# A four-layer graph-attention kernel: the end of layer 2 without its division, other forms of small VectorE operations, and mean rows taken elsewhere

## The chip, the cores and the metric

The kernel runs on one core of one Trainium2 chip. The time is that of one execution on the device in microseconds, and the figure for a kernel is the median of its runs. A separate execution is recorded by the hardware profiler; all views of the profile come from that one.

The engines appear under these names: PE (TensorE, matrix products), PEld (its weight loads), DVE (VectorE), ACT (ScalarE), POOL (GpSimd) and SP (SyncE, which issues most DMAs). Each engine works through its own queue in order and waits at an instruction whose inputs are not there.

## The reference

Eight graphs' worth of node features `x` (8 × 2048 × 64) pass through four attention layers over one sparse 2048 × 2048 adjacency. Each layer adds its output to `x`, and reads `h = max(layernorm(x), 0)`:

```python
h = jnp.maximum(_layernorm(x, axis=-1), 0.0)
x = x + _L0_gnn_ref(h, adj)          # dot-product attention over h
h = jnp.maximum(_layernorm(x, axis=-1), 0.0)
x = x + _L1_gnn_ref(h, adj, W, a)    # additive attention, then elu
h = jnp.maximum(_layernorm(x, axis=-1), 0.0)
x = x + _L2_gnn_ref(h, adj, Wh, bh, Wo, bo, gamma, beta)
h = jnp.maximum(_layernorm(x, axis=-1), 0.0)
x = x + _L3_gnn_ref(h, adj, W, a)    # additive attention, then relu
```

Layer 2 has two attention steps. The second of them is what the text below calls "layer 2's end":

```python
h = jnp.einsum('bnc,hdc->bhnd', x, Wh)
out_h = _gat_layer(h, mask[None, None], bh[None, :, None, :])   # 4 heads
z = jax.nn.leaky_relu(cat, negative_slope=0.2)
h2 = jnp.einsum('bnk,dk->bnd', z, Wo)
out2 = _gat_layer(h2, mask[None], bo)                 # softmax(h2 h2^T) h2 + bo
z2 = jax.nn.leaky_relu(out2, negative_slope=0.2)
mu = jnp.mean(z2, axis=-1, keepdims=True)
var = jnp.mean(jnp.square(z2 - mu), axis=-1, keepdims=True)
out = (z2 - mu) * jax.lax.rsqrt(var + LN_EPS) * gamma + beta
```

## The kernel before

The nodes are cut into 16 tiles of 128. A row holds all eight batches of a node: 8 × 64 = 512 values (`F` = 512, `B` = 8, `D` = 64), so a tile is 128 x 512 in fp32. The graph is sparse, so the kernel first makes lists of neighbours from the adjacency (`lists`, in layer 0's stage), and each layer gathers the neighbours' rows from a table in DRAM by indirect DMA (`gather`, L244, issued by POOL) into a ring of 26 slots. A tile has `ROWS[i]` slots in which every node has its own neighbour and `PACKED[i]` slots in which the remaining edges of all its nodes are packed together. There are 49 and 32 of these, 81 in all. For packed slots two selection matrices, `sel` and its transpose `selt`, say to which node an edge belongs. `sel` is made in layer 0, stored to DRAM and, at layer 2's end, loaded back as one DMA of 2 MB (L880).

Each layer is a `pipeline` of stages over the tiles. Stages of different tiles are written out interleaved, and the framework's scheduler orders each engine's queue further by a timeline of its own. Buffers rotate (`bufs=`), so a stage can run ahead only as far as they allow.

The stages that matter for the change:

- `norm_a` and `norm_b` are the layer norm. `norm_a` sums the rows on DVE (L261), makes the mean (L265) and subtracts it (L268), both on an engine given as `eng`, and has ACT square the result. `norm_b` sums the squares (L281), and ACT makes the inverse root as exp(−0.5 · ln(q/D + eps)).
- `pre_c` makes the normalised row `xh` (ACT, eight instructions a tile, L292) and transposes it on PE (L300) with a copy by ACT (L301). `pre_d` multiplies it with `u` (L343) and stores the row to the next layer's table (`store_rows`, L352). For tables 0, 1 and 4, `store_rows` also adds the tile to a mean row: products with `ones` (L357), a DVE addition to `acc` (L361), and after the last tile a transpose, a copy and a DMA to row N of the table. The gathers of the next layer wait for all rows of the table, the mean row included.
- `scores` multiplies the query rows with gathered rows and sums over each head (L423, L425, L431, L432, all DVE). `exps` takes the exponentials on ACT (L437).
- `weigh_sum` multiplies the gathered rows with the weights, on POOL in layer 0 and at layer 2's end (L381), and sums the slots on PE into `y` in PSUM (L386).

At layer 2's end, `second3` adds up the weights S and takes 1/S (L902, L903). `third3` multiplies y by 1/S (L472), adds the bias `bo` (L910), takes the leaky relu (L445, L446) and starts the layer norm. `fourth3` scales (L292), multiplies by gamma (L918), adds beta (L919), adds x (L486), stores x, and starts the next layer's norm on DVE. At the end `bounds` keeps the largest S, which later decides whether the result is within the limits of this method.

In layer 0, POOL has the mean and the centring of the norm (L265, L268), the addition of the attention's result to x (L480), `weigh_sum` and the gathers. In the two additive layers (1 and 3) `weigh_sum` is on DVE, and POOL has the gathers and little more.

Of the kernel before, what the change touches and what calls it, by code (L numbers as in the profile page):

```python
# [65 lines left out]
def edge_stack(ctx: ExitStack, tc: tile.TileContext, x_in, adj, w1, w1t, a1, wh, wht, bh, wo, bo,  # L66
# [28 lines left out]
    nc.gpsimd.memset(eps, EPS)  # L95
    ones = const.tile([P, 1], F32, name="ones")
# [17 lines left out]
    acc = const.tile([P, F // P], F32, name="acc")  # L114

# [40 lines left out]
    bo_b, gamma_b, beta_b = (const.tile([P, D], F32, name=name) for name in ("bo_b", "gamma_b", "beta_b"))  # L156

    def weights_in(pool):
# [34 lines left out]
        for t, src in ((bo_b, bo), (gamma_b, gamma), (beta_b, beta)):  # L193
            nc.gpsimd.dma_start(out=t, in_=bass.AP(tensor=src.tensor, offset=src.offset, ap=[[0, P], [1, D]]))
# [60 lines left out]
    def rows_of(k, i):  # L255
        return table[k][i * P:(i + 1) * P, :F]

    def norm_a(src, st, centre, eng=nc.vector):
# [4 lines left out]
        if centre:  # L263
            mean = small.tile([P, B], F32, name="ln_m")
            eng.tensor_scalar(mean, s, INV_D, None, op0=OP.mult)  # L265
            st["less"] = None
            st["src"] = rows_pool[0].tile([P, F], F32, name="ln_xc", bufs=3)
            eng.tensor_tensor(heads(st["src"]), heads(src), wide(mean), op=OP.subtract)  # L268
# [4 lines left out]
        nc.vector.tensor_scalar(st["less"], s, -INV_D, None, op0=OP.mult)  # L273
# [4 lines left out]
    def norm_b(st):  # L278
# [3 lines left out]
        nc.scalar.activation(q, q, AF.Ln, scale=INV_D, bias=eps)  # L282
# [12 lines left out]
    def transposed(src):  # L295
# [5 lines left out]
        nc.scalar.copy(t.rearrange("p k n -> p (k n)"), p)  # L301
# [5 lines left out]
    def pre_c(u, eng=None):  # L307
        def f(i, st):
# [6 lines left out]
            if u is not None:  # L315
                st["xt"] = transposed(st["xh"])
# [19 lines left out]
    def pre_d(k, u):  # L336

        def f(i, st):
# [8 lines left out]
            store_rows(k, i, xh, k != 2)  # L347
        return f

    def store_rows(k, i, xh, mean):  # L350
        cols = table[k].shape[1]
        nc.sync.dma_start(out=table[k][i * P:(i + 1) * P, :], in_=xh[:, :cols])  # L352
        if mean:
            C = F // P
            p = ps_m.tile([P, F], F32, name="m")
            for c in range(C):
                nc.tensor.matmul(p[:, c:c + 1], xh[:, c * P:(c + 1) * P], ones, start=True, stop=True)  # L357
            if i == order[0]:
                nc.vector.tensor_copy(acc, p[:, :C])
            else:  # L360
                nc.vector.tensor_tensor(acc, p[:, :C], acc, op=OP.add)  # L361
            if i == order[-1]:
                p = ps_m.tile([P, F], F32, name="m")
                nc.tensor.transpose(p[:C, :P], acc, ident)
                mr = rows_pool[0].tile([C, P], F32, name="mr", bufs=1)
                nc.vector.tensor_copy(mr, p[:C, :P])
                nc.sync.dma_start(out=table[k][N, :F].rearrange("(c p) -> c p", p=P), in_=mr)

# [4 lines left out]
    def weigh_sum(i, st, w, own=None, eng=nc.gpsimd):  # L373
# [1089 lines left out]
```

## Time and profile before

| | us |
|---|---|
| median of 3 runs (1598.85 to 1601.07) | 1600.91 |
| the profiled execution | 1596.83 |
| its span, from first to last instruction | 1595.0 |

Busy time in the span:

| engine | busy us | share | instructions |
|---|---|---|---|
| PE | 1295.0 | 81% | 4280 |
| DVE | 1242.0 | 78% | 2489 |
| POOL | 1006.4 | 63% | 844 |
| ACT | 768.0 | 48% | 2475 |

The stages follow one another, because each layer gathers from a table that needs every tile of the layer before:

| stage | from to (us) | PE | DVE | ACT | POOL |
|---|---|---|---|---|---|
| start, lists and layer 0 | 0 to 366 | 284.4 | 294.7 | 181.3 | 233.4 |
| layer 1 | 366 to 600 | 191.0 | 179.2 | 150.5 | 82.7 |
| layer 2, four heads | 600 to 1152 | 477.8 | 429.7 | 264.6 | 454.7 |
| layer 2's end | 1152 to 1440 | 215.5 | 241.5 | 152.7 | 159.9 |
| layer 3 | 1440 to 1595 | 126.3 | 96.9 | 18.9 | 75.6 |

How to read the lines of the profile in this document: a group's line has the source line, the engine and operation, the tile written and the tiles read, the shape, the number of instructions, their busy time in us and the mean duration of one in ns. After the second bar stands the engine's idle time just before these instructions, with what ended most of it. A timeline line begins with the start in us and the duration. A busy PE is not PE at its peak, as matrix products are pipelined and their ends are modelled. An fp32 product shows as two records. "issue" is time in which an engine waited for nothing that the profile shows.

### The profile page before, as it was taken

How to read it: one execution, taken by the hardware profiler on the slowest of the kernel's cores; microseconds unless marked ns; L12 is line 12 of the kernel's file. 1: busy time of each engine (PE TensorE's matmuls, PEld its weight loads, DVE VectorE, ACT ScalarE, POOL GpSimd, SP SyncE). 2: the span in 40 equal slices, each digit the busy share in tenths (PEclk: the TensorE clock that was granted, in tenths of full speed). 3: DMA queues.
4: the chain of work that ended last, by engine and by line, in shares of the span. 5: the costliest groups of instructions: out<-in, count | busy, mean ns of one | idle time of the engine just before them, and what ended most of it. 6: DMA issues, size and time to landing. Idle time of an engine off the chain costs nothing.

```text
span 1595.0 us, 16633 instructions
## 1 busy us (share of the span) xinstructions
PE 1295.0 (81%) x4280; PEld 671.0 (42%) x4280; DVE 1242.0 (78%) x2489; ACT 768.0 (48%) x2475; POOL 1006.4 (63%) x844
## 2 busy tenths in 40 slices
PE   3768898995989771899987999999747788975888
PEld 1624354564544430344343444443323354563555
DVE  5998989854689776999998799871159999974666
ACT  3424555672557781465541455555424446680111
POOL 6336777766750007998789889898278486306650
PEclk9997887987999996899999999999968798957899
DMA  7775654536874449465266345400085354136761
GB/s 216 233 244 158 201 183 152 198 107 182 260 253 153 173 164 348 161 232 173 88 209 204 111 141 182 158 14 7 27 321 154 93 179 126 67 103 204 244 205 69
DMA packets 88177, 266.99 MB, mean 167 GB/s; under 512 B 14957, under 2 KB 15001, under 8 KB 79881
## 3 DMA queue, kind: packets, MB, share of 16 engines
q0 software_dynamic: 37392, 141.05, 28.3%
q1 hardware_dynamic: 50680, 124.80, 22.6%
q8 instruction: 36, 0.59, 0.2%
q14 instruction: 69, 0.56, 0.1%
HBM read 208.74 MB, written 57.05 MB: 167 GB/s over the span
## 4 chain that ended last, share of the span: by engine, by line
PE 24%; DVE 13%; POOL 8%; DMA 7%; ACT 6%; issue 5%; SPq 0%; POOLq 0%; DVEq 0%; ACTq 0%
PE y L809 10%; DMA g<-table,idx 4%; POOL wh L794 3%; POOL g L244 3%; DMA rows<-table 3%; PE y L386 3%; PE y L801 2%; PE m L846 2%; ACT yn L817 2%; PE m L858 2%; DVE s L781 2%; DVE prod L777 2%; DVE prod L423 1%; POOL wh L807 1%; PE m L842 1%
## 5 line engine op out<-in xcount | busy, mean ns | idle before, releaser
L244 POOL DMA_INDIRECT g<-table,idx x405 | 389.3, 961 | 268.3 <-issue 115.6
L794 POOL TENSOR_TENSOR wh<-g,w 128x1024 f32<-128x1024 f32 x162 | 307.2, 1918 | 35.8 <-PE y L809 33.9
L386 PE MATMUL y<-wg,ident 128*128 128x512 f32 x392 | 223.0, 696 | 22.6 <-POOL wg L381 12.7
L381 POOL TENSOR_TENSOR wg<-g,w 128x1024 f32<-128x1024 f32 (+1 forms) x91 | 156.6, 1736 | 75.2 <-ACT w L437 65.9
L781 DVE TENSOR_REDUCE s<-prod 128x32 f32<-128x2048 f32 x81 | 183.9, 2286 | 20.2 <-ACT w L783 19.8
L809 PE MATMUL y<-wh,ident 128*128 128x512 f32 x320 | 155.6, 614 | 23.7 <-POOL wh L807 21.5
L386 PE MATMUL y<-wg,selt 128*128 128x512 f32 x256 | 135.1, 634 | 4.6 <-POOL wg L381 2.9
L809 PE MATMUL y<-wh,selt 128*128 128x512 f32 x256 | 123.1, 605 | 13.2 <-POOL wh L794 13.2
L817 ACT ACTIVATE yn<-y,rec 128x64 f32<-128x64 f32 x512 | 111.3, 367 | 29.7 <-PE y L809 29.0
L386 PEld LDWEIGHTS y<-wg,ident 128*128 128x128 f32 x392 | 79.0, 219 | 106.6 <-issue 66.2
L777 DVE TENSOR_TENSOR prod<-q,g 128x2048 f32<-128x2048 f32 x49 | 111.5, 2275 | 3.7 <-ACT g L775 3.3
L381 DVE TENSOR_TENSOR wg<-g,w 128x1024 f32<-128x1024 f32 (+1 forms) x92 | 98.9, 1086 | 11.3 <-PE y L386 9.5
L443 DVE SCALAR_TENSOR_TENSOR zt<-m,bhc,att 128x512 f32<-128x512 f32 x64 | 47.1, 737 | 75.3 <-ACT att L442 75.3
L809 PEld LDWEIGHTS y<-wh,ident 128*128 128x128 f32 x320 | 59.4, 195 | 98.6 <-issue 62.4
L400 PE MATMUL m<-w,selt 128*128 128x8 f32 (+1 forms) x384 | 58.8, 255 | 50.7 <-ACT w L437 16.5
L400 PEld LDWEIGHTS m<-w,selt 128*128 128x128 f32 x384 | 60.8, 205 | 92.9 <-ACT w L437 26.8
L775 ACT COPY g<-g 128x512 f32<-128x512 f32 x81 | 50.4, 622 | 84.5 <-DVE prod L777 83.6
L429 PE MATMUL q<-rows,sel 128*128 128x512 f32 x128 | 79.8, 725 | 12.7 <-DVE prod L431 4.7
L801 PE MATMUL y<-rows,ident 128*128 128x512 f32 x128 | 70.9, 640 | 19.6 <-DMA rows<-table 14.4
L777 DVE TENSOR_TENSOR prod<-qe,g 128x2048 f32<-128x2048 f32 x32 | 73.0, 2281 | 13.9 <-DMA qe<-qtab,qidx 12.7
L357 PE MATMUL m<-ones,xh 128*128 128x1 f32 x384 | 70.6, 307 | 10.7 <-DVE idx L717 3.5
L357 PEld LDWEIGHTS m<-ones,xh 128*128 128x128 f32 x384 | 70.8, 274 | 20.0 <-issue 13.2
(221 smaller groups left out, 2673.0 us busy)
## 6 DMA issues: line engine op xcount, KB each, us to landing
qtab<-q SPq DMA_DIRECT2D x16, 1040.0 KB, 4.1
a<-in_adj_dram SPq DMA_DIRECT2D x32, 512.0 KB, 5.1
q<-qtab SPq DMA_DIRECT2D x14, 1040.0 KB, 5.3
table<-xh SPq DMA_DIRECT2D x48, 256.0 KB, 3.3
rows<-table SPq DMA_DIRECT2D x48, 256.0 KB, 4.1
xs<-x SPq DMA_DIRECT2D x48, 256.0 KB, 2.2
x<-xs SPq DMA_DIRECT2D x48, 256.0 KB, 3.3
table<-xh SPq DMA_DIRECT2D x32, 260.0 KB, 2.1
```

What stands on the lines that cost most here:

```text
L244: g = nc.gpsimd.indirect_dma_start(out=ring[:, (held[i] + t) % RING, :cols], out_offset=None, in_=table[k][:, :], in_offset=bass.IndirectO ...
L357: nc.tensor.matmul(p[:, c:c + 1], xh[:, c * P:(c + 1) * P], ones, start=True, stop=True)
L381: eng.tensor_tensor(wg[:, :m].rearrange("p t (b d) -> p t b d", b=B), g[:, :, :F].rearrange("p t (b d) -> p t b d", b=B), w[:, t0:t0 + m, ...
L386: nc.tensor.matmul(y, lhs(i, t), wg[:, t - t0, :], start=(t == 0 and own is None), stop=(t == n - 1))
L400: nc.tensor.matmul(p[:, :cols], selt(i, t), packed[:, t, :], start=(t == 0), stop=(t == T - 1))
L429: nc.tensor.matmul(qe, sel(i, t - K), q, start=True, stop=True)
L777: nc.vector.tensor_tensor(pr.rearrange("p (b h) d -> p b h d", h=H), q[:, :B * H * D].rearrange("p (b h d) -> p b h d", h=H, d=D), heads(g ...
L781: nc.vector.tensor_reduce(s[:, t - lo, :], pr, AX.X, OP.add)
L794: nc.gpsimd.tensor_tensor(wg, heads(row(i, t))[:, :, None, :].to_broadcast([P, B, 2, D]), w[:, :, 2 * k:2 * k + 2, None].to_broadcast([P, ...
L801: nc.tensor.matmul(st["ys"][j], ident, xb[:, 4 * j:4 * j + 4], start=True, stop=False)
L809: nc.tensor.matmul(st["ys"][j], lhs(i, t), wg[:, 4 * j:4 * j + 4], start=False, stop=(t == n - 1))
L817: nc.scalar.activation(yn[:, b, h, :], st["ys"][j][:, b, h, :], AF.Copy, scale=st["rec"][:, 4 * j + b, 2 * k + h:2 * k + h + 1])
```

## The change

It has four parts.

1. **Form.** On DVE, small `tensor_scalar` and `tensor_tensor` operations whose operands lie in SBUF become `scalar_tensor_tensor`, with a constant tile (`zero`, `np1`, `neg1`, each 128 x 1, read as a broadcast) as the second tensor. This touches the lists of layer 0, the mean and the centring of the norm where they are on DVE, one subtraction at layer 2's end and two operations of the additive layers.
2. **Layer 2's end.** The softmax is no longer divided by S before the layer norm. The layer norm of S·v equals that of v when the eps inside is scaled by S². So `bo` is added as S·bo, by one more product on PE: S is transposed, copied to SBUF, and multiplied with a block matrix `bo_d` (8 x 512), which a DMA and a selection on POOL make at the start of the stage. eps·S² takes the place of eps in `norm3`. Beta is added to x on POOL, before the result is added; the next layer's mean and centring go to POOL.
3. **Selection matrices.** `sel` is loaded by tile in `take3` instead of whole.
4. **Mean rows.** They move from `store_rows` to `pre_c`. For table 1 the ACT copy of each transposed row becomes four, each with its sum as a second output, and one reduction follows after the last tile. For table 4 one product with `ones` as the stationary operand sums 512 columns over all tiles in one PSUM buffer. Table 0 is summed as before.

```diff
+    zero, np1, neg1 = (const.tile([P, 1], F32, name=name) for name in ("zero", "np1", "neg1"))
+    for t, v in ((zero, 0.0), (np1, N + 1.0), (neg1, NEG)):
+        nc.gpsimd.memset(t, v)
...
+    def alike(t, like):
+        return t.to_broadcast(like.shape)
+
+    def times(dst, src, k):
+        nc.vector.scalar_tensor_tensor(dst, src, k, alike(zero, src), op0=OP.mult, op1=OP.add)
+
+    def less_from(dst, src):
+        nc.vector.scalar_tensor_tensor(dst, src, -1.0, alike(np1, src), op0=OP.mult, op1=OP.add)
...
-            eng.tensor_scalar(mean, s, INV_D, None, op0=OP.mult)
+            if eng is nc.vector:
+                times(mean, s, INV_D)
+            else:
+                eng.tensor_scalar(mean, s, INV_D, None, op0=OP.mult)
...
-            eng.tensor_tensor(heads(st["src"]), heads(src), wide(mean), op=OP.subtract)
+            if eng is nc.vector:
+                nc.vector.scalar_tensor_tensor(heads(st["src"]), heads(src), 1.0, wide(mean), op0=OP.mult,
+                                               op1=OP.subtract)
+            else:
+                eng.tensor_tensor(heads(st["src"]), heads(src), wide(mean), op=OP.subtract)
...
-    def norm_b(st):
+    def norm_b(st, more=None):
...
-        nc.scalar.activation(q, q, AF.Ln, scale=INV_D, bias=eps)
+        if more is None:
+            nc.scalar.activation(q, q, AF.Ln, scale=INV_D, bias=eps)
+        else:
+            nc.vector.scalar_tensor_tensor(q, q, INV_D, more, op0=OP.mult, op1=OP.add)
+            nc.scalar.activation(q, q, AF.Ln)
...
-        nc.scalar.copy(t.rearrange("p k n -> p (k n)"), p)
+        if part is None:
+            nc.scalar.copy(t.rearrange("p k n -> p (k n)"), p)
+        else:
+            for k in range(F // P):
+                nc.scalar.activation(t[:, k, :], p[:, k * P:(k + 1) * P], AF.Copy, accum_out=part[:, k:k + 1])
...
-                st["xt"] = transposed(st["xh"])
+                st["xt"] = transposed(st["xh"], parts[:, i, :] if k == 1 else None)
+            if k is not None:
+                mean_of(k, i, st["xh"])
...
+    def mean_of(k, i, xh):
+        if k == 4:
             if i == order[0]:
+                kept["mean"] = ps_w[0].tile([P, F], F32, name="w")
+            p = kept["mean"]
+            nc.tensor.matmul(p[:1, :], ones, xh[:, :F], start=(i == order[0]), stop=(i == order[-1]))
             if i == order[-1]:
+                mr = rows_pool[0].tile([1, F], F32, name="mr", bufs=1)
+                nc.vector.tensor_copy(mr, p[:1, :])
+                nc.sync.dma_start(out=table[k][N:N + 1, :F], in_=mr)
+            return
+        C = F // P
+        if k == 1:
+            if i == order[-1]:
+                nc.vector.tensor_reduce(acc, parts.rearrange("p i c -> p c i"), AX.X, OP.add)
...
+        if more is not None:
+            nc.tensor.matmul(y, *more, start=False, stop=False)
...
-                nc.vector.tensor_scalar(ends, ends, LIFT, 0.0, op0=OP.subtract, op1=OP.max)
+                nc.vector.scalar_tensor_tensor(ends, ends, LIFT, alike(zero, ends), op0=OP.subtract, op1=OP.max)
...
-                nc.vector.tensor_scalar(idx[:, at + K:at + K + T], ke, -1.0, N + 1.0, op0=OP.mult, op1=OP.add)
-                nc.vector.tensor_scalar(mp, mp, NEG, None, op0=OP.mult)
+                less_from(idx[:, at + K:at + K + T], ke)
+                times(mp, mp, NEG)
...
-        nc.sync.dma_start(out=sel_all[0], in_=sel_dram[:, :])
+
+        bo_d = rp.tile([B, F], F32, name="bo_d", bufs=1)
+        nc.sync.dma_start(out=heads(bo_d), in_=bass.AP(tensor=bo.tensor, offset=bo.offset, ap=[[0, B], [0, B], [1, D]]))
+        nc.gpsimd.affine_select(out=heads(bo_d), in_=heads(bo_d), compare_op=OP.is_equal, fill=0.0, base=0,
+                                pattern=[[-1, B], [0, D]], channel_multiplier=1)
 
         def take3(i, st):
             gather(3, i, st)
             load(st, "rows", rows_of(3, i), 5)
+            mine = slice(POFF[i] * P, (POFF[i] + PACKED[i]) * P)
+            nc.sync.dma_start(out=sel_all[0][:, mine], in_=sel_dram[:, mine])
...
-            nc.vector.scalar_tensor_tensor(seen[:, i, :], p, 1.0, d, op0=OP.add, op1=OP.add)
-            nc.vector.reciprocal(rec, seen[:, i, :])
-            st["y"] = weigh_sum(i, st, w, st["rows"])
+            S = seen[:, i, :]
+            nc.vector.scalar_tensor_tensor(S, p, 1.0, d, op0=OP.add, op1=OP.add)
+            nc.vector.scalar_tensor_tensor(rec, S, EPS, S, op0=OP.mult, op1=OP.mult)
+            p = ps_m.tile([P, F], F32, name="m")
+            nc.tensor.transpose(p[:B, :P], S, ident)
+            sums = small.tile([B, P], F32, name="sums")
+            nc.scalar.copy(sums, p[:B, :P])
+            st["y"] = weigh_sum(i, st, w, st["rows"], more=(sums, bo_d))
             done(i, st)
 
         def third3(i, st):
-            y = st["y"]
-            divide(st, y)
-            nc.vector.tensor_tensor(heads(y), heads(y), over_d(bo_b), op=OP.add)
             t = rows_pool[0].tile([P, F], F32, name="z2", bufs=4)
-            leaky_max(t, y, rows_pool[0].tile([P, F], F32, name="att"))
+            leaky_max(t, st["y"], rows_pool[0].tile([P, F], F32, name="att"))
             norm_a(t, st, True)
...
-            nc.vector.tensor_tensor(heads(p), heads(p), over_d(beta_b), op=OP.add)
-            add_store(i, st, p, True)
-
-        pipeline(take3, first3, second3, third3, both(pre_b, xs_rows), fourth3, pre_b, pre_c(u3), pre_d(4, u3))
+            add_store(i, st, p, True, eng=nc.gpsimd)
+
+        def norm3(i, st):
+            norm_b(st, st["rec"])
+
+        def beta3(i, st):
+            nc.gpsimd.tensor_tensor(heads(st["x"]), heads(st["x"]), over_d(beta_b), op=OP.add)
+
+        pipeline(take3, first3, second3, third3, both(norm3, xs_rows, beta3), fourth3, pre_b, pre_c(u3, None, 4), pre_d(4, u3))
         bounds(4, seen)
+        nc.vector.tensor_scalar(most[:, 4:5], most[:, 4:5], 1e15, None, op0=OP.mult)
```

Left out: the same exchange of forms at the other places of the lists and in the additive layers, and the load of `bo_b`, which goes.

## The prediction

> **What bounds the kernel now.** I read the page's forty slices first, to split the program into stages, then the busy time of each engine by stretch, then the groups of the stage that the change touches most, then single rows. In the slices a digit is a tenth of 39.9 us.
>
> ```profile
> DVE  5998989854689776999998799871159999974666
> POOL 6336777766750007998789889898278486306650
> ```
>
> Digits 1 to 8 are layer 0 with the edge lists, 10 to 14 layer 1, 15 to 28 the four-head half of layer 2, 29 to 35 (1152 to 1439 us) layer 2's end, the rest layer 3. Layer 2's end has a row of nines on DVE, while POOL has eights beside fours and a three. By stretch (columns: PE, PEld, DVE, ACT, POOL, each busy us and instructions; clock; DMA share; GB/s):
>
> ```profile
> 1152.00:1196.00 44.00, 18.26 (x42) 9.37 (x43) 21.59 (x45) 9.57 (x25) 30.44 (x31) 0.65 0.84 301
> 1196.00:1240.00 44.00, 34.09 (x83) 14.82 (x82) 39.86 (x74) 21.62 (x63) 35.21 (x28) 0.85 0.51 152
> 1240.00:1280.00 40.00, 30.00 (x88) 15.50 (x88) 36.96 (x56) 17.61 (x68) 21.05 (x15) 0.74 0.30 93
> 1320.00:1360.00 40.00, 33.62 (x108) 17.99 (x107) 40.00 (x79) 27.16 (x102) 24.44 (x18) 0.87 0.36 112
> 1360.00:1400.00 40.00, 35.92 (x161) 22.16 (x160) 40.00 (x89) 28.18 (x100) 13.60 (x9) 0.96 0.21 73
> ```
>
> From 1196 to 1400 DVE has almost no hole: the stage is DVE-bound. PE's busy figure is pipelined and modelled, and its idle time there ends mostly on POOL. Before 1196 the DMA limits (84%, 301 GB/s), and POOL issues one gather each 1.25 us. The groups of that stage (busy us, mean ns, then idle before):
>
> ```profile
> L268 DVE TENSOR_TENSOR ln_xc<-x,ln_m 128x512 f32<-128x512 f32 x16 | 12.3, 767 | 0.1
> L472 DVE TENSOR_TENSOR y<-y,rec 128x512 f32<-128x512 f32 x16 | 11.0, 690 | 2.4 <-PE y L386 2.4
> L918 DVE TENSOR_TENSOR q<-q,gamma_b 128x512 f32<-128x512 f32 x16 | 11.0, 688 | 1.8 <-ACT q L292 1.8
> L919 DVE TENSOR_TENSOR q<-q,beta_b 128x512 f32<-128x512 f32 x16 | 11.0, 688 | 0.0
> L910 DVE TENSOR_TENSOR y<-y,bo_b 128x512 f32<-128x512 f32 x16 | 11.0, 688 | 0.0
> L244 POOL DMA_INDIRECT g<-table,idx x82 | 80.7, 985 | 94.5 <-issue 47.1 <-DMA table<-mr 40.4 <-POOL wg L381 2.1
> L381 POOL TENSOR_TENSOR wg<-g,w 128x1024 f32<-128x1024 f32 x35 | 68.0, 1954 | 54.9 <-ACT w L437 50.9 <-PE y L386 3.8
> ```
>
> The change deletes L472, L910, L919 and the DVE form of L268 for x. POOL has about 61 us of waits in front of L381 (54.9 + 6.0 for the 128x512 form), nearly all for weights that DVE makes late.
>
> **What a page states, against this trace.** The Trainium skill, "SBUF — State Buffer", section "Who interferes with whom", says that a DVE instruction in a two-port mode or with two SBUF inputs excludes a GpSimd instruction that reads SBUF; one waits for the other to end. This decides the edit of forms. The trace agrees:
>
> ```profile
> 266.44 3.75 DVE L664 TENSOR_SCALAR mba<-ell 128x3 f32<-128x3 f32 x1
> 42.85 1.04 POOL L268 TENSOR_TENSOR ln_xc<-x,ln_m 128x512 f32<-128x512 f32 x1
> 43.45 0.99 DVE L313 SCALAR_TENSOR_TENSOR xh<-ln_xc,ln_r 128x512 f32<-128x512 f32 x1
> ```
>
> L664 works on three elements and usually takes 157 ns (its median); here it ends just after three POOL operations running into each other have ended at 270.15. L313 has the form the change introduces, with two SBUF inputs: it starts while POOL works, usually takes 680 ns, and takes 990; two other L313 that start under a POOL operation end 547 to 548 ns after it ends, as this one does. So I take it that SCALAR_TENSOR_TENSOR with a broadcast constant from SBUF waits just as TENSOR_SCALAR does. One-element TENSOR_SCALARs do not wait now (L664 at 193.48 and 252.12, under POOL, took 136 and 144 ns); with a second SBUF operand they would.
>
> **The change part by part**, against the profiled execution (1596.8 us, span 1595.0). The median shown is 4.1 us higher; I add that at the end.
>
> *Layer 2's end, DVE.* Removed per tile: three 128x512 passes, one x centring, a mean, a reciprocal (191 ns) and the mean-row add (152 ns). Summed: 11.0 × 3 + 12.3 + 3.0 (half of L265's 6.0) + 3.1 + 2.3 = 53.7 us. Added: two 128x8 operations per tile (eps·S² and its addition before Ln), 32 × 0.16 = 5. Net 49 us of busy time. Neighbours overlap by nearly 0.09 us (starts 0.60 apart at 0.69 long), so about 40 us of DVE time.
>
> *Layer 2's end, POOL.* Added per tile: mean 0.233, centring 1.046 (both rows of POOL in layer 0), adding beta, priced as L480 there (1.271): 2.55 × 16 = 41 us. POOL's work is now 80.7 + 79.6 + about 17 of pauses between gathers = 177, and becomes 218. DVE falls from 242 to about 193. **POOL becomes the longer queue.** The stage takes 284 us from first gather (1155.1) to next layer's first (1439.0): 177 work, 61 waits, 40 after the last POOL operation (1398.6), the rest small. After: 218 + waits + about 12, since POOL centres the last tile itself late in the chain. Waits should shrink, as DVE delivers weights sooner, but not go: the 17-slot tile 0 alone costs 16.8 now, and POOL's queue will also stand behind row sums (L261). Layer 0 has the same mix on POOL, and there the waits before its four tensor groups sum to 27 us. I take 32: 218 + 32 + 12 = 262, **22 less**. Behind a waiting POOL stand gathers and the next tile's wg, so PE and DVE wait for it in turn.
>
> *More collisions.* POOL tensor time goes from 79 to 120 us, and each tile keeps five exposed small DVE operations. Today 7.5 us over norm are lost so in this stage; twice the time with POOL busy, and less clustering, makes about 20: 12 more, on DVE only. DVE's 193 + 12 stays below 218.
>
> *PE and ACT there.* Added: a transpose of S (0.36), an 8x128 copy (0.17 to 0.28), one 512-column product (0.65); removed: eight mean-row products a tile counted by record (0.285 each in 128 records = 21 us), replaced by a wide one in two records. PE within 5 us: no bound. The product of sums and bias stands ahead of the slots' products on PE and waits for S, transpose, copy: about 1 us per tile, beside POOL's wg. Zero, unless PE leads POOL.
>
> *Selection matrices by tile.* The 2 MB load (8.2 us to land) is split; before tiles 13, 12, 11, 10, 9, 8 only 0.5 MB is needed. First rows land about 5 us sooner. POOL's gather pace still rules to 1188, so I count 0 in the likeliest case, 4 if DVE is the bound. The new bias load with a POOL selection ahead of the gathers may cost 0 to 3; I take 1 inside the rounding. SP gets some 16 issues of 0.32 us, beside other work.
>
> *Mean rows.* Layer 4's: today the add, transpose, copy and store follow the rows' store; the gather at 1438.98 waits for it. Afterwards the rows' store (1434.4, 2.1 to land) is last: 2.4 us, contained in the 262. Layer 0's: PE loses 1.84 us per tile; ACT's 0.58 copy becomes four 128x128 with an accumulator. No row shows that; 4 × 0.25 (the pitch of L292) to 4 × 0.47; I take 1.3. In the tail PE is serial (transposes 1.09, copy, products 1.87, mean row 1.84): shorter by about 1 per tile for two tiles, and the last step (gather 365.17) about 2: **4 less**.
>
> *Form of small operations.* By the rule above nothing is won. Fourteen one-element operations while POOL is busy in layer 0 newly wait, at the 0.45 us average of their longer siblings (17.6 us over norm in 39): 6 us of DVE, 90% busy there: **5 more**. Bound below: see the third case. In layers 1 and 3 POOL has hardly a tensor operation; 0.
>
> Sum: −22 − 4 + 5 = −21: 1575.8, and with 4.1: **1580 us**.
>
> **Rivals.** *DVE stays the bound*: POOL's waits vanish into its work. For it: 61 us of waits are a consequence of DVE's pace. Against: its sum exceeds DVE's. Stage −40 + 12 − 4 − 2.4 = −34; −34 − 4 + 5: 1568.
> *The new form does not wait for POOL*: small operands might differ from L313's 512 elements. Then L645, L662, L664, L717, L718 lose 23.5 us over norm, two thirds on the path (16), plus 5 in layer 2's end and no penalty of 5: −22 − 4 − 21: 1554.
> *POOL's queue takes it all back*: POOL's waits stay at 61, because its in-order steps now wait for DVE sums between two wg. 218 + 61 + 12 = 291, 7 more; with form 5 and other queues' gain 4: +8, and some 3 if the selection of the bias delays the first gather: 1612. It decides from waits above 54 us.
> *No net effect*: the gains meet waits of about 50: 1600.
>
> **How the numbers follow.** Chances: forecast 0.45 (own range 1568 to 1592), DVE bound 0.17, form free 0.10, POOL takes it back 0.22, none 0.06. A measurement can tell about 0.2% (3 us) from no change. Faster 0.72, same 0.06, slower 0.22. Range 1557 to 1606: it leaves out half of the third and of the fourth case.
>
> **What would show it.** Layer 2's end should have POOL at eights and nines and DVE at seven or eight; L472 there, L910 and L919 on DVE gone; the stage 262 long. TENSOR_SCALAR outliers of layer 0 should return as SCALAR_TENSOR_TENSOR outliers of 0.5 to 3 us. If the latter are absent, the page's rule was misapplied. If POOL idles over 54 us in front of its tensor operations, the fourth case holds.

## The result, and the profile after

| | before | after |
|---|---|---|
| median, same chip (us) | 1599.88 (1598.71 to 1601.07) | 1624.84 (1621.06 to 1627.91) |
| ratio, 95% interval | | 1.0155 [1.0127, 1.0183] |
| profiled execution, span | 1596.8, 1595.0 | 1627.2, 1625.4 |

The changed kernel is slower by 25 us. Cut at the first gather of each layer, the two traces differ mainly in one stage:

| stage (us) | start | layer 0 | layer 1 | layer 2, heads | layer 2's end | layer 3 |
|---|---|---|---|---|---|---|
| before | 76.8 | 288.3 | 230.6 | 559.4 | 283.9 | 156.0 |
| after | 75.9 | 290.7 | 233.0 | 560.3 | 308.5 | 157.0 |

So 24.6 of the 30 us between the profiled spans lie in layer 2's end, which was to become 22 us shorter. In the slices of the page, each 40.6 us long, it is digits 29 to 37, the first and the last in part:

```profile
DVE  5997988845689776999996899841479958954666
POOL 5436777857740027997789888987387586526650
```

POOL has no row of eights and nines there, and DVE's row of nines has holes. By stretch (columns as in the same view of before):

```profile
1200.00:1240.00 40.00, 23.02 (x44) 8.60 (x44) 34.28 (x41) 16.31 (x50) 33.51 (x29) 0.73 0.50 145
1280.00:1320.00 40.00, 35.60 (x110) 17.56 (x110) 26.99 (x49) 18.28 (x72) 28.02 (x24) 0.80 0.41 130
1320.00:1360.00 40.00, 28.90 (x63) 11.13 (x62) 32.77 (x42) 16.14 (x50) 35.48 (x31) 0.88 0.45 133
```

Where DVE had almost no hole before, it is 67 to 86% busy in these three stretches and POOL 70 to 89%: neither is the bound, each waits in turn. The POOL groups of the stage (busy us, mean ns, then the idle time before and what ended it):

```profile
L433 POOL TENSOR_TENSOR wg<-g,w 128x1024 f32<-128x1024 f32 x35 | 66.7, 1916 | 14.8 <-PE y L438 6.5 <-ACT w L489 3.6 <-ACT xh L316 3.0
L988 POOL TENSOR_TENSOR x<-x,beta_b 128x512 f32<-128x512 f32 x16 | 20.2, 1269 | 7.5 <-DMA x<-xs 7.4
L433 POOL TENSOR_TENSOR wg<-g,w 128x512 f32<-128x512 f32 x11 | 11.5, 1044 | 15.3 <-ACT w L489 10.2 <-PE y L438 4.7 <-issue 0.2
L281 POOL TENSOR_SCALAR ln_m<-ln_s 128x8 f32<-128x8 f32 x16 | 3.7, 232 | 39.3 <-DVE ln_s L274 30.2 <-DVE ln_q L305 4.4 <-DVE s L956 2.8
```

The largest single wait is new. POOL now makes the mean of the next layer's norm (L281), 3.7 us of work in all, and waits 39.3 us in front of it, mostly for DVE's row sums (L274). The gathers and weighings of later tiles stand behind. In front of the weighings themselves (L433, both forms) POOL waits 30.1 us, where it waited 60.9 before. So part of the waiting has only moved to another instruction, and the 39.3 us are not all added time. And on DVE:

```profile
L285 DVE SCALAR_TENSOR_TENSOR ln_xc<-z,ln_m 128x512 f32<-128x512 f32 x16 | 21.5, 1344 | 0.8 <-DVE ln_m L266 0.5
L965 DVE SCALAR_TENSOR_TENSOR rec<-seen 128x8 f32<-128x8 f32 x16 | 14.2, 886 | 0.1
L305 DVE SCALAR_TENSOR_TENSOR ln_q<-ln_q,rec 128x8 f32<-128x8 f32 x16 | 14.1, 882 | 0.2
```

L965 and L305 are the two new operations on eight values a partition (eps·S², and its addition before Ln). They were priced at 0.16 us and average 0.88. L285, the centring of the layer norm's input, takes 1.34. Before, in its old form, it took 0.73:

```profile
L268 DVE TENSOR_TENSOR ln_xc<-z,ln_m 128x512 f32<-128x512 f32 x16 | 11.7, 733 | 0.0
```

The timeline shows the worst case of L965; POOL and then DVE over the same 7 us (start, duration):

```profile
1352.23 1.05 POOL L288 TENSOR_TENSOR ln_xc<-x,ln_m 128x512 f32<-128x512 f32 x1
1353.23 3.75 POOL L433 TENSOR_TENSOR wg<-g,w 128x1024 f32<-128x1024 f32 x2
1356.95 1.25 POOL L988 TENSOR_TENSOR x<-x,beta_b 128x512 f32<-128x512 f32 x1
1358.36 0.99 POOL L248 DMA_INDIRECT g<-table,idx  x1 [0.16 <-POOL x L988]
```
```profile
1352.38 5.85 DVE L965 SCALAR_TENSOR_TENSOR rec<-seen 128x8 f32<-128x8 f32 x1
1358.16 0.69 DVE L981 TENSOR_TENSOR q<-q,gamma_b 128x512 f32<-128x512 f32 x1
```

One operation on 8 values a partition stands from 1352.4 to 1358.2, through four tensor operations of POOL that follow each other without a gap, and ends when the last of them does.

For all kernels below I worked out the same figures of this stage from the records. **Lost** is the time of DVE's tensor operations over the usual duration of their shape (0.16 us for 8 columns, 0.68 for 512, 1.22 for 1024), counted where it is above 0.1 us. The length of the stage is the sum of the last three columns: POOL's work with its pauses between gathers, its waits in front of tensor operations, and what comes after its last operation.

| kernel | stage | DVE busy | of it lost | DVE idle | POOL work | POOL waits | tail |
|---|---|---|---|---|---|---|---|
| before | 283.9 | 241.5 | 7.7 | 42.3 | 182.6 | 60.8 | 40.4 |
| after | 308.5 | 237.2 | 39.8 | 71.3 | 218.9 | 77.6 | 12.0 |

DVE's work without the loss fell from 234 to 197 us, as it should. But 32 us more are lost behind POOL, and 29 more idle.

### The profile page after: what moved, and what is told of

Read it like the earlier page. It is cut to its first block, busy times and chain, and to the rows that moved or that the text cites. A ratio compares the mean times of both kernels' runs of the same rounds, so it can differ in the third digit from the quotient of the medians.

```text
span 1625.4 us, 16350 instructions
## 1 busy us (share of the span) xinstructions
PE 1316.1 (81%) x4103; PEld 643.8 (40%) x4103; DVE 1233.6 (76%) x2394; ACT 778.6 (48%) x2604; POOL 1047.6 (64%) x895
## 5 line engine op out<-in xcount | busy, mean ns | idle before, releaser
L848 POOL TENSOR_TENSOR wh<-g,w 128x1024 f32<-128x1024 f32 x162 | 307.1, 1917 | 35.3 <-PE y L863 33.3
L438 PE MATMUL y<-wg,ident 128*128 128x512 f32 x392 | 227.7, 709 | 22.6 <-POOL wg L433 13.2
L433 POOL TENSOR_TENSOR wg<-g,w 128x1024 f32<-128x1024 f32 (+1 forms) x91 | 155.4, 1719 | 39.6 <-ACT w L489 19.2
L438 PE MATMUL y<-wg,selt 128*128 128x512 f32 x256 | 140.8, 656 | 4.4 <-DVE wg L433 3.3
L871 ACT ACTIVATE yn<-y,rec 128x64 f32<-128x64 f32 x512 | 110.8, 366 | 30.9 <-PE y L863 30.1
L433 DVE TENSOR_TENSOR wg<-g,w 128x1024 f32<-128x1024 f32 (+1 forms) x92 | 98.8, 1086 | 10.7 <-PE y L438 8.2
L855 PE MATMUL y<-rows,ident 128*128 128x512 f32 x128 | 70.9, 640 | 20.6 <-DMA rows<-table 15.6
L357 PE MATMUL q<-q,xt 128*128 128x512 f32 x128 | 67.3, 637 | 17.3 <-DVE prod L359 11.0
L900 PE MATMUL m<-att,whd 128*128 128x512 f32 x128 | 67.9, 612 | 9.8 <-ACT att L898 9.7
```

Source lines behind the costliest of these rows:

```text
L433: eng.tensor_tensor(wg[:, :m].rearrange("p t (b d) -> p t b d", b=B), g[:, :, :F].rearrange("p t (b d) -> p t b d", b=B), w[:, t0:t0 + m, ...
L438: nc.tensor.matmul(y, lhs(i, t), wg[:, t - t0, :], start=(t == 0 and own is None), stop=(t == n - 1))
L848: nc.gpsimd.tensor_tensor(wg, heads(row(i, t))[:, :, None, :].to_broadcast([P, B, 2, D]), w[:, :, 2 * k:2 * k + 2, None].to_broadcast([P, ...
L855: nc.tensor.matmul(st["ys"][j], ident, xb[:, 4 * j:4 * j + 4], start=True, stop=False)
L871: nc.scalar.activation(yn[:, b, h, :], st["ys"][j][:, b, h, :], AF.Copy, scale=st["rec"][:, 4 * j + b, 2 * k + h:2 * k + h + 1])
L900: nc.tensor.matmul(p, whd[j // 2], yt, start=True, stop=True)
```

## The experiments

Four theories. **L**: DVE operations with two inputs in SBUF (and TENSOR_SCALAR with one) stand behind POOL's tensor operations. **F**: the form itself is to blame. **Q**: POOL's in-order queue waits for DVE sums and makes PE and DVE wait in turn. **O**: the scheduler's order of the kernel before is a lucky one, and any edit draws another.

**One part of the change at a time** (each on the kernel before):

```diff
f1_forms: only the forms
-        nc.vector.tensor_scalar(st["less"], s, -INV_D, None, op0=OP.mult)
+        times(st["less"], s, -INV_D)
f2_end: only layer 2's end
-            divide(st, y)
-            nc.vector.tensor_tensor(heads(y), heads(y), over_d(bo_b), op=OP.add)
+            st["y"] = weigh_sum(i, st, w, st["rows"], more=(sums, bo_d))
f3_sel: only the loads of sel
-        nc.sync.dma_start(out=sel_all[0], in_=sel_dram[:, :])
+            nc.sync.dma_start(out=sel_all[0][:, mine], in_=sel_dram[:, mine])
f4_mean: only the mean rows
-            store_rows(k, i, xh, k != 2)
+            store_rows(k, i, xh)
+                mean_of(k, i, st["xh"])
```

> Before with part 1 alone (forms of small VectorE operations). Theory L (small VectorE operations with two SBUF inputs stand behind GpSimd's tensor operations) expects the outliers of layer 0 to return in the new form and the whole to be 0 to 8 us slower, +5 us in the middle, and layer 2's end unchanged at 284 us within 4. Theory F (the loss comes from the new form itself, as layer 2's end uses it too) expects +15 us or more, most of it in layer 2's end.

> Before with part 2 alone (layer 2's end without the division, old forms of mean and centring). Theories L and Q (Q: GpSimd's in-order queue, standing at sums that VectorE makes late) both expect nearly the whole loss here: layer 2's end 300 to 312 us against 284, the program +16 to +28 us. Theory F or a loss by parts 3 and 4 expect less than +10 us.

> Before with part 3 alone (selection matrices by tile). All theories expect the first rows of layer 2's end to land about 5 us sooner and the time to change by -5 to +1 us. A loss of more than 4 us would mean that the added DMAs disturb SyncE's queue.

> Before with part 4 alone (mean rows at the transposes). The prediction's step expects -4 us in layer 0 and -2.4 us at the end of layer 2, together -6 us. A theory that four ACT copies per tile are too slow expects 0 to +6 us in layer 0, where the last tiles wait for them.

| kernel | ratio to before | layer 0 | layer 2's end | lost | DVE idle | POOL work | POOL waits | tail |
|---|---|---|---|---|---|---|---|---|
| f1_forms | 1.0124 [1.0091, 1.0157] | 303.4 | 301.6 | 20.0 | 47.5 | 181.8 | 71.9 | 48.0 |
| f2_end | 1.0223 [1.0175, 1.0270] | 300.6 | 306.4 | 30.0 | 78.3 | 220.0 | 74.5 | 11.9 |
| f3_sel | 1.0061 [1.0040, 1.0081] | 290.2 | 299.8 | 20.1 | 45.5 | 180.3 | 73.1 | 46.4 |
| f4_mean | 1.0110 [1.0082, 1.0137] | 289.1 | 301.9 | 17.5 | 51.8 | 182.3 | 73.0 | 46.5 |

Every part alone is slower, and their excesses add up to 5.2%, three times that of the whole. f3_sel is the odd one: it gives DVE and POOL exactly the old work and still lengthens the stage by 16 us (in a profiled execution of 1612.76 us, where its nine runs lie between 1605.65 and 1616.33). Its POOL group, where the same group of before had 54.9 us of idle time in front:

```profile
L381 POOL TENSOR_TENSOR wg<-g,w 128x1024 f32<-128x1024 f32 x35 | 66.8, 1920 | 67.6 <-ACT w L437 57.9 <-DVE q L919 5.1 <-PE y L386 4.4
```

So the parts don't have a cost each that adds up. Likewise layer 0 is 12 us longer in f2_end, which changes nothing in that layer but one small load at the start. f1_forms met the number that F had expected, 15 us or more, and not L's 0 to 8. But 15 us of it lie in layer 0, which is no longer than 290.7 in the changed kernel with the same forms, and layer 2's end is as long in f3_sel and f4_mean, which have no new form. That speaks for O, beside L. For f3_sel another cause was named ahead, that the added loads disturb SyncE's queue. It was not tried alone; n_rows6 below is as slow without any added load.

**Three tests of O that change no work**, all on the kernel before: the load of `sel` in two pieces, in four, and one more buffer for the gathered rows. **Two of L and Q** on the changed kernel.

```diff
n_halves (n_quarters: four pieces)
-        nc.sync.dma_start(out=sel_all[0], in_=sel_dram[:, :])
+        for c in (0, half):
+            nc.sync.dma_start(out=sel_all[0][:, c:c + half], in_=sel_dram[:, c:c + half])
n_rows6
-            load(st, "rows", rows_of(3, i), 5)
+            load(st, "rows", rows_of(3, i), 6)
q_dve, on the changed kernel: beta and the next layer's norm of x back on DVE
-            add_store(i, st, p, True, eng=nc.gpsimd)
+            nc.vector.tensor_tensor(heads(p), heads(p), over_d(beta_b), op=OP.add)
+            add_store(i, st, p, True)
g_lockfree, on the changed kernel: no second SBUF input in the operations of DVE's norm there
-            leaky_max(t, st["y"], rows_pool[0].tile([P, F], F32, name="att"))
-            norm_a(t, st, True)
+            leaky_max(y, y, rows_pool[0].tile([P, F], F32, name="att"))
...
+            nc.vector.scalar_tensor_tensor(heads(st["src"]), wide(s), INV_D, heads(y), op0=OP.mult, op1=OP.subtract)
...
+            nc.scalar.activation(st["sqz"][:, :, D], seen[:, i, :], AF.Square, scale=(EPS * D) ** 0.5)
```

In g_lockfree the leaky relu stays in PSUM, the mean is folded into the centring, and ACT writes eps·D·S² as a 65th column beside the 64 squares, so that one row sum on DVE does what L965 and L305 did. That leaves DVE three small operations a tile fewer. POOL's work is kept.

> Before with the 2 MB load of the selection matrices issued as two loads of 1 MB, otherwise the same instructions. Theory O (the scheduler's order of before is a favourable draw at layer 2's end, and any edit there draws another) expects layer 2's end at 295 to 305 us against 284, VectorE's loss behind GpSimd there at 15 to 25 us against 8, and the program +10 to +20 us. If parts 1, 3 and 4 lost by what they do, this one is the same as before within 3 us.

> The changed kernel with the small VectorE operations of z's norm rid of their second SBUF input: eps times S squared is made by ACT as a 65th column of the squares, the leaky relu stays in PSUM, the mean goes into the centring. Same result. GpSimd keeps all its new work. Theory L (VectorE's operations standing behind GpSimd's) expects VectorE's loss at layer 2's end to fall from 40 to below 15 us and the stage from 308 to 270-285, the program to 1585-1603. Theory Q (GpSimd's in-order queue) expects the stage to stay at 300 or more, the program at 1615 or more. Theory O alone expects anything within 8 us of the changed kernel.

> The changed kernel with beta and the next layer's mean and centring back on VectorE; the division stays out. Theory Q expects the stage to fall to 280 or less and the program below 1600. Theory L expects VectorE's loss to fall from 40 to about 20 us as GpSimd's tensor time falls from 119 to 79 us, but 26 us of work come back: stage 295 to 305, program 1612 to 1622.

> The kernel before with the one load of the selection matrices at layer 2's end issued as four; no other work is changed, but the order in which the framework's scheduler queues the instructions comes out differently. If the order of before is one draw out of a spread (O), layer 2's end comes out anywhere in 284 to 302 us, with 8 to 20 us of excess on VectorE; if each part of the change costs by what it does, 284 to 288 us and an excess of 7 to 12, and the kernel 1598 to 1604.

> The kernel before with six buffers in place of five for the gathered rows of layer 2's end: no work is changed, and gathers can start one tile earlier. O: another draw, layer 2's end in 284 to 302 us. If the parts cost by what they do: 280 to 286 us, the kernel 1596 to 1602.

| kernel | ratio to before | layer 2's end | lost | DVE idle | POOL work | POOL waits | tail |
|---|---|---|---|---|---|---|---|
| n_halves | 0.9990 [0.9976, 1.0004] | 286.3 | 11.9 | 41.0 | 182.1 | 63.9 | 40.3 |
| n_quarters | 1.0109 [1.0055, 1.0163] | 306.6 | 16.7 | 56.9 | 181.5 | 79.4 | 45.7 |
| n_rows6 | 1.0164 [1.0113, 1.0215] | 304.6 | 19.3 | 51.4 | 182.0 | 76.4 | 46.3 |
| q_dve | 1.0052 [1.0023, 1.0081] | 295.4 | 23.3 | 54.7 | 181.2 | 78.8 | 35.3 |
| g_lockfree | 1.0054 [1.0028, 1.0079] | 287.9 | 6.3 | 88.4 | 217.2 | 58.6 | 12.1 |

n_quarters and n_rows6 have two runs each, in a series in which the kernel before took 1645.6 us. In the four kernels profiled in that series, layers 1 and 3 are together 40 to 50 us longer than in the profile of before above, which is about the 45 us, so the lengths of layer 2's end should stand within some us. The ratios compare with the kernel before in the same series.

**O holds as a spread, not as a rule.** n_halves stays where the kernel before is, against what O had expected of it, and the other two, which do the same work with the same instructions, are 1.1 and 1.6% slower, with the stage near 305 us. With f3_sel and f4_mean, whose work in this stage is the same or a little less, that makes four of six orders at 300 to 307 and two at 284 to 286.

**L holds for the lost time.** Without second SBUF inputs, 33 of the 40 lost us are gone, and the stage is 20.6 us shorter at the same POOL work. That is near the 270 to 285 us that L had expected and far from Q's 300 or more. The edit also draws a new order, though, so not all of the 20.6 us need be L's. The changed kernel itself and the two orders of it below, which keep the loss, have stages of 300 to 308.5 us. What is left of the loss in g_lockfree is mostly one line that kept both inputs in SBUF (L954), while the centring of z, now with one input in PSUM, takes its plain 0.68 us under the same POOL:

```profile
L978 DVE SCALAR_TENSOR_TENSOR ln_xc<-ln_s,y 128x512 f32<-128x512 f32 x16 | 10.9, 678 | 2.9 <-ACT xh L316 2.6
...
L954 DVE SCALAR_TENSOR_TENSOR s<-s,c 128x24 f32<-128x24 f32 x6 | 5.9, 980 | 0.0
```

**Q is not shown as a cost.** In q_dve, POOL has no mean to wait for, and its waits are 78.8 us in all, as long as in the changed kernel (77.6); all of them now stand in front of the weighings. Its 295.4 us and its loss of 23.3 are what L had expected; Q had expected 280 us or less. In g_lockfree DVE is idle for 88 us, while POOL still waits in front of its mean:

```profile
L281 POOL TENSOR_SCALAR ln_m<-ln_s 128x8 f32<-128x8 f32 x16 | 3.7, 232 | 29.2 <-DVE ln_s L274 28.2
```

PE is a rival that no run tests. It is now the busiest engine of the stage, with 241.7 of 287.9 us by its modelled figure. The chain of work that ended last lies on PE for 136 us of this stage, where in the kernel before it lay on DVE for 120 and on PE for 44.

**Taking those waits away.** gx_dve is g_lockfree with the next layer's mean and centring back on DVE, and only beta left on POOL. gxp_psum does the same with x summed in PSUM and copied to SBUF by ACT, which also makes the mean.

```diff
gx_dve, on g_lockfree
-            norm_a(x, st, True, nc.gpsimd)
+            norm_a(x, st, True)
gxp_psum, on g_lockfree
-            nc.vector.scalar_tensor_tensor(x, p, -1.0, x, op0=OP.mult, op1=OP.add)
+            nc.vector.scalar_tensor_tensor(p, p, -1.0, x, op0=OP.mult, op1=OP.add)
+            nc.scalar.copy(x, p)
...
+            nc.scalar.mul(mean, s, INV_D)
...
+            nc.vector.tensor_tensor(heads(st["src"]), heads(p), wide(mean), op=OP.subtract)
```

> g_lockfree with the norm's centring of the next layer's x (16 tiles) put back from GpSimd to VectorE; GpSimd keeps only the addition of beta. What remained idle in g_lockfree (VectorE 88 us, GpSimd about 88 us in layer 2's end) was GpSimd waiting for VectorE's row sums and VectorE waiting in turn for GpSimd's tiles. If those mutual in-order waits set the rest (Q), layer 2's end falls from 287.9 to 265 to 280 us, although VectorE's work grows by about 20 to 25 us, and the kernel takes 1590 to 1602 us. If standing behind GpSimd's operations (L) is all, the centring has two SBUF inputs and stands behind GpSimd again: excess of VectorE rises from 6 to 12 to 20 us, and the stage stays at 284 to 300, the kernel at 1604 to 1618.

> As gx_dve, but the sum of the new x stays in PSUM (ScalarE copies it to SBUF and makes the mean), so that no VectorE operation of the next layer's x norm has two SBUF inputs. L: the excess of VectorE in layer 2's end stays at 5 to 9 us. If both L and Q hold, the stage is 260 to 276 us and the kernel 1582 to 1598 us, the fastest of all. If it's ScalarE that is late next (some 16 more copies of a tile at about 0.6 us and 16 means), the stage stays at 280 to 290.

| kernel | ratio to before | layer 2's end | lost | DVE idle | POOL work | POOL waits | tail |
|---|---|---|---|---|---|---|---|
| gx_dve | 0.9969 [0.9953, 0.9986] | 281.0 | 13.7 | 62.4 | 197.9 | 47.9 | 35.2 |
| gxp_psum | 0.9972 [0.9951, 0.9993] | 280.5 | 4.8 | 71.9 | 196.9 | 47.9 | 35.7 |

Both beat both kernels, if only by 0.3% of the kernel before. Both ran in the series at 1645.6 us, so only the ratios compare with the first group. POOL's weighings in gx_dve:

```profile
L433 POOL TENSOR_TENSOR wg<-g,w 128x1024 f32<-128x1024 f32 x35 | 66.4, 1909 | 27.3 <-PE y L438 16.9 <-ACT ln_sz L981 4.9 <-PE m L965 2.4
L433 POOL TENSOR_TENSOR wg<-g,w 128x512 f32<-128x512 f32 x11 | 11.5, 1049 | 11.9 <-PE y L438 11.9
```

The wait of 29.2 us in front of the mean is gone, but the waits fall by only 10.7 us in all, from 58.6 to 47.9: those in front of the weighings rise from 24.2 to 39.2, most of them for PE. POOL's work falls by 19, and the tail gives back 23, since DVE again centres the last tiles. The stage is just above the 265 to 280 us that Q had expected and the loss of 13.7 within L's 12 to 20, so this run doesn't decide between them. gxp_psum loses 9 us less behind POOL than gx_dve and is no faster, where 260 to 276 us had been expected. What took the gain isn't separated: ACT has 9 us more work (165 of 280 us busy), and the 280 us are also what had been expected of an ACT that is late.

**What part is the order's, what the change's?** a_rows6 is the changed kernel with the edit of n_rows6; a0_noform is the changed kernel with all forms of before; p_before and p_after are both kernels with their instructions queued in the order in which the program is written.

```diff
a_rows6, on the changed kernel
-            load(st, "rows", rows_of(3, i), 5)
+            load(st, "rows", rows_of(3, i), 6)
a0_noform, on the changed kernel
-        times(st["less"], s, -INV_D)
+        nc.vector.tensor_scalar(st["less"], s, -INV_D, None, op0=OP.mult)
p_before, p_after
-    with tile.TileContext(nc, schedule_with_timeline_sim=True) as tc:
+    with tile.TileContext(nc) as tc:
```

> The changed kernel with six buffers in place of five for the gathered rows of layer 2's end: no work is changed, only the scheduler's order (the same edit took the kernel before up by 1.6%). If the 40 us that the changed kernel's VectorE loses behind GpSimd, and its stage of 308 us, are its work's own (L), it loses 30 to 48 us again and the stage is 302 to 316 us, ratio to before 1.012 to 1.024. If they were an unlucky draw (O), the loss is under 25 and the stage under 298, ratio under 1.010.

> The changed kernel with the form of the small VectorE operations undone, so that only the rest of the change is in it. L: the operations that stood behind GpSimd at layer 2's end are mostly new ones or had two SBUF inputs before (the small ones of the end without division, the centring), so the loss falls by no more than 8 us, to 28 to 42, and the stage is 298 to 310. F (the form is to blame): the loss falls to under 20, the stage to under 292. Layer 0: within 5 us of the changed kernel's 291.

> The kernel before with its instructions queued in the order in which the program writes them, without the framework's scheduler. Its own time is open: 1600 to 1900 us. It serves as the base for p_after: with both in written order, no draw of the scheduler stands between them.

> The changed kernel in the order in which the program writes its instructions. If the change itself lengthens layer 2's end (L and Q), its stage is longer than p_before's by 8 to 30 us and its VectorE loses 10 to 35 us more there. If only the scheduler's draw did (O), the stage is within 5 us of p_before's, or shorter by up to 20 as the prediction had it.

| kernel | median | ratio to before | layer 0 | layer 2's end | lost | DVE idle | POOL work | POOL waits | tail |
|---|---|---|---|---|---|---|---|---|---|
| a_rows6 | 1622.95 | 1.0123 [1.0095, 1.0152] | 288.1 | 305.0 | 34.7 | 72.4 | 219.4 | 73.1 | 12.5 |
| a0_noform | 1619.61 | 1.0121 [1.0060, 1.0181] | 290.6 | 299.9 | 31.3 | 70.5 | 218.9 | 69.1 | 11.9 |
| p_before | 1771.84 | 1.1050 [1.1020, 1.1081] | 374.3 | 337.4 | 18.4 | 83.7 | 179.9 | 107.9 | 49.6 |
| p_after | 1734.89 | 1.0839 [1.0806, 1.0871] | 346.8 | 322.0 | 41.7 | 84.3 | 218.3 | 89.9 | 13.8 |

The loss belongs to the change: 31 to 42 us in the changed kernel, a_rows6, a0_noform and p_after, 8 to 20 in every order of the old work. One other order moved the changed kernel little (a_rows6). On this draw the two new operations averaged 0.56 and 0.51 us, and POOL's mean waited as long:

```profile
L281 POOL TENSOR_SCALAR ln_m<-ln_s 128x8 f32<-128x8 f32 x16 | 3.7, 233 | 39.8 <-DVE ln_s L274 24.7 <-ACT q L316 8.2 <-DVE ln_q L305 4.8
```

F explains at most the 8.6 us between after and a0_noform in this stage, where two orders of the changed kernel differ by 3.5 anyway; the intervals of the ratios overlap. The old form is no way out: in a0_noform the mean on DVE is a TENSOR_SCALAR with one input again, and it waits too, in this order even more than the new form did (0.42 us on average in the changed kernel):

```profile
L266 DVE TENSOR_SCALAR ln_m<-ln_s 128x8 f32<-128x8 f32 x16 | 11.7, 731 | 0.2
```

In written order the sign turns: the change is 37 us faster. The two stages by window (layer 0, layer 2's end), p_before and then p_after:

```profile
76.20:450.50 374.30, 283.53 (x864) 148.59 (x869) 250.49 (x939) 157.68 (x536) 195.41 (x175) 0.77 0.44 142
1266.00:1603.40 337.40, 235.28 (x707) 127.65 (x707) 253.66 (x460) 152.41 (x529) 157.06 (x127) 0.73 0.38 124
```
```profile
76.40:423.10 346.70, 249.71 (x738) 121.28 (x741) 252.98 (x921) 165.81 (x649) 195.92 (x174) 0.83 0.48 154
1235.80:1557.80 322.00, 241.21 (x658) 106.99 (x658) 237.72 (x381) 150.90 (x545) 197.97 (x176) 0.80 0.41 130
```

The two profiled executions, 1778.14 and 1731.26 us, lie further apart than the medians, so the lengths overstate the difference by some us. Neither of p_after's alternatives fits alone: the stage is 15 us shorter, as O had it, though DVE loses 23 us more, as L had it. There POOL's waits start from 108 and fall by 18; in the scheduled kernel they start from 61 and rise by 17. This fits a change that removes idle time which the scheduler's order had already removed; that reading is argued from these two pairs, not tried apart.

## Why the prediction was wrong

*Layer 2's end, POOL* is the step that failed, and in it one term: "I take 32" for the waits. It measured 77.6. The two other terms came out: 218 of work against 218.9, "about 12" after the last operation against 12.0. 218.9 + 77.6 + 12.0 = 308.5, the stage. The 218 are partly luck: counted in the same way, POOL's work before was 182.6, not 177, and it rose by 36, not 41. The term of the waits was wrong in sign: "Waits should shrink, as DVE delivers weights sooner". In front of the weighings they did shrink, from 60.9 to 30.1. Over all of POOL's tensor operations they rose by 16.8. The runs show three causes at work, and not the share of each:

- DVE lost more than forecast. *More collisions* said about 20 us; it is 39.8. By the groups shown, L965 and L305 lost 23 us of it (16 times 0.73 and 0.72) and L285 11. Scaling up the 7.5 us of before missed that a small operation can wait through a whole run of POOL operations. With these operations rewritten the waits are 58.6 and the stage 287.9 (g_lockfree, in an order of its own).
- The mean put a wait of 39.3 us into POOL's queue, mostly for DVE's sums. The prediction named that ("stand behind row sums (L261)") and left it inside the 32. It took its size from layer 0's 27, which was no guide to this stage. How much it adds is open, as waits move along an in-order queue: without it they are 10.7 us less in gx_dve and none less in q_dve.
- The 61 us of before were themselves low. Four other orders of about the same work have 73 to 79, and a stage 16 to 23 us longer. The prediction took the order as given; what in it is better (which swap) I didn't find out.

How much of the 24.6 us is the order's, how much the change's, can only be bounded. Against the four other orders of the old work the changed kernel's stage is 2 to 9 us longer; without the forms it would be about even with f3_sel; in written order it is shorter by 15. If those four are the usual case, some 16 to 23 us are the old order's luck, which the change could not keep. No run puts the change into the old order, so that stays an estimate.

*DVE in that stage*: "Net 49 us of busy time", "about 40 us of DVE time". The work fell by 36.4 (241.5 − 7.7 to 237.2 − 39.8). But the longer of two queues is no bound when each waits for the other: DVE idles 71 us and POOL waits 78.

*Fourth rival* ("POOL's queue takes it all back", from waits above 54 us): its own test is met, at 77.6, and its reason, steps that "wait for DVE sums", is the largest row of waits, though their net cost is open. It took the waits as unchanged at 61, so its 291 us for the stage fell short by 17.5. *DVE stays the bound* is refuted by DVE's 71 idle us. *Form free* is refuted too, by the row below.

*Form*: the rule was applied rightly. Of 139 one-value operations in layer 0, 34 ran beside a POOL tensor operation before, and none of these took more than 0.16 us. In the changed kernel three lose 5.5 us. That this meets the forecast of 6 is luck, which was 14 times 0.45. One of the three, DVE and then POOL:

```profile
258.47 4.23 DVE L717 SCALAR_TENSOR_TENSOR mba<-ell,neg 128x1 f32<-128x1 f32 x1
```
```profile
258.90 3.77 POOL L433 TENSOR_TENSOR wg<-g,w 128x1024 f32<-128x1024 f32 x2
```

It starts before the POOL pair that it waits for; a gather (257.94 to 258.89) was running then. The price of "5 more" is not seen in the stage, though: layer 0 is 290.7 with the forms and 290.6 without. Layer 0's whole loss is even less than before (18.2 against 22.9).

*Mean rows*: "4 less" in layer 0 did not come: f4_mean has 289.1 us there against 288.3. The last step did get shorter. From the issue of the last row's store to the next layer's first gather it was 4.57 us before and is 2.91 in f4_mean and 3.00 after (4.59, 3.08 and 3.05 at layer 2's end), where 2 and 2.4 us less were forecast. PE's busy time in layer 0 fell by 6.4 us in the changed kernel, and a copy with its sum takes ACT 0.25 us, 1.0 for the four of a tile where 1.3 was taken (start, duration):

```profile
318.53 0.29 ACT L329 ACTIVATE xt<-q 128x128 f32<-128x128 f32 x1
318.69 0.23 ACT L329 ACTIVATION_READ_ACCUMULATOR xt<-q 128x1 f32 x1
318.78 0.30 ACT L329 ACTIVATE xt<-q 128x128 f32<-128x128 f32 x1
```

So this step is on the path, and the rest of the layer took its gain back. Whether the order did that isn't separated. *Selection by tile* at 0 to 4: no gain is seen; f3_sel is slower, which the orders above make likely to be the order's doing.

*PE within 5* was off: in layer 2's end PE rose from 215 to 244 us by the modelled figure. The product of sums and bias was priced at 0.65 us a tile, about one record; it has two, 1.24 us together:

```profile
L430 PE MATMUL y<-bo_d,sums 8*128 8x512 f32 x32 | 19.8, 701 | 0.8 <-ACT sums L969 0.7
```

The transpose of S adds 4.7 us. The wide product of the mean row (L389) takes 21.4 us, no less than the products that it replaces (L357, 21.0). Whether PE then bounds part of the stage, no run tests.

The Trainium skill's "SBUF — State Buffer", section "Who interferes with whom", was borne out for what it states: DVE operations with two SBUF inputs stand behind POOL's reads, with one in PSUM they don't (L978, 0.68 us where L285 took 1.34). What I took from it was too mild: the two new operations of 8 values, priced at 0.16 us, averaged 0.88 in a stage in which POOL's tensor operations follow one another.

## What to carry to other kernels

Price a small VectorE operation with two SBUF inputs by the run of GpSimd tensor operations that it may meet, not by its size, and keep one of its inputs in PSUM, or let ScalarE do it. Before work is moved onto an in-order queue, list what each moved instruction waits for, but don't read the wait in front of it as its cost: 3.7 us of means had 39 us of waits in front of them, and taking the means and the centring off again left POOL's waits the same in one run and 11 us shorter in another. And when a scheduler reorders the queues, first make one or two edits that change no work: here they alone moved the kernel by up to 1.6%, more than three of the four parts under test.

## What was unexpected of the hardware

- In these traces a VectorE operation that waits for GpSimd was not let in between GpSimd tensor operations that follow each other closely: one waited through four, 5.85 us for 0.16 of work.
- The kernel before took 1600.94 us in one series of runs on the chip numbered 3, and 1645.62 us in another 20 minutes later under the same number. In the four kernels profiled in the later series, layers 1 and 3 were longer by 18 to 25 us each, at the same busy times of DVE, ACT and POOL. The cause is open.
